# Cross-attention over 64 sequences: stores issued by ScalarE, fetches reordered on SyncE, the turn of the queries moved, the last scores in other PSUM banks

## The chip, the cores and the metric

The kernel runs on one core of a Trainium2 chip. The metric is the device time of one execution in microseconds. Five engines have instruction queues of their own: TensorE (PE, with its weight loads as PEld), VectorE (DVE), ScalarE (ACT), GpSimd (POOL) and SyncE (SP). SP and ACT also issue DMA transfers; SPq and ACTq in the profile are these issues.

## The reference

All is float32. x is 64 x 256 x 512, ctx is 64 x 256 x 384, the hidden width is 512.

```python
text_p  = einsum('bld,dh->blh', x, W_text)   + b_text
audio_p = einsum('bsd,dh->bsh', ctx, W_audio) + b_audio
Q = layer_norm(text_p, g1, beta1)
K = layer_norm(audio_p, g2, beta2)
V = audio_p
alpha = softmax(einsum('blh,bsh->bls', Q, K) / sqrt(512), axis=-1)
h = einsum('bls,bsh->blh', alpha, V)
h = einsum('blh,hk->blk', h, W_out) + b_out
return layer_norm(h + x, g_out, beta_out)
```

layer_norm takes mean and variance over the last axis, with 1e-5 added to the variance.

## The kernel before

**Work per sequence.** For each of the 64 sequences b (256 text rows and 256 audio rows, each as two tiles of 128 partitions) the kernel makes:

- the text projection q and the audio projection k. For b = 0 and 1 they are plain products (`multiply`, L314, product L317). For b from 2 on they are cut into blocks (class `Blocks`): seven products of block sums instead of eight products (`products`, L427), taken out of PSUM and added together by DVE (`leave`, one for each product, L438: the "sums" of the prediction). POOL makes the sums of the inputs (`sum_x`, `sum_c`, L271 to L289). A pool `p_pj` of four PSUM banks holds the products; two products share a bank.
- the LayerNorm of q and k without gain and shift: the squares (ACT, `square`, L335), 1/sqrt (POOL, `scales`, L297 and L299), the scaling of the rows (ACT, `normalise`, L363 or L365).
- the turn of the rows, so that the hidden axis lies on the partitions: the rows are stored to DRAM (`store`, L373, tiles qd and kd, 512 KB), fetched back as 32-wide squares (`fetch`, four DMAs of 128 KB by `squares`, L88, tiles qq and kq), and turned by DVE within 32 x 32 squares (`turn`: L91 for q, L394 for k). ACT applies gain and shift there (`affine`, L401, four instructions), giving qT and kT.
- the scores of 256 x 256 (L463) into a bank of `p_at` (two banks), their maxima (DVE, L473), the exponentials (ACT, L480). The exponentials take the same way through DRAM: stored as ed (`store_e`, L494, 256 KB), fetched in squares as eq (L88, 4 x 64 KB), turned by DVE (`turn_e`, L91).
- the context z = alpha times ctx (L525, two banks of `p_at` in turn, copied to zT by ACT, L532) and the output y (L542, into `p_y`, two banks), for which W_audio and W_out have been multiplied together beforehand (wao, `fold_multiply`, with the bias bao by `fold_bias`). DVE takes y out of PSUM and adds x (`evict`, L551), and does the last LayerNorm (`shift` L565, `settle` L570); the output rows are stored (L580).

x and ctx are loaded twice: as rows (`load_rows`, x 512 KB, c 384 KB) and as squares for the projections (`load_squares`, xq 4 x 128 KB, cq 4 x 96 KB; `turn_x`, `turn_c` on DVE).

**Order.** The order of every engine's queue is the order in which the code is written (`manual_schedule`, L65); nothing is rearranged. An engine works through its queue in order and waits where an operand or a buffer isn't ready. SP's queue holds all DMAs except the rows of biases and gains (`row`, L127) and five small vectors (`load_columns`), which ACT issues.

**The loop** (L693 to L771, b from 0 to 61) handles scores of b, context and output of b-1, the end of the LayerNorm of b-2, the projections of b+2, the squares of b+3 and b+4. In SP's order an iteration is: qq and kq of b+1 (L697, L698), ed of b, eq of b, xq and cq of b+4, x and c of b+1, the output of b-2, qd of b+2, kd of b+2. On DVE the turn of q[b+1] (L725) stands between sums 5 and 3 of the text projection; on PE all seven text products, the context of b-1 and the audio products follow each other, in the banks of `p_pj` and `p_at` that DVE and ACT empty.

**Before the loop** (L610 to L690) the weights are loaded and folded, the first two sequences are projected by plain products, and `turn_rows` (L167) turns c_0 and x_0 on PE. **After it** (L774 to L827) the last two sequences are finished; there the exponentials are turned on PE (`transpose_e`, L504).

Of the kernel before, what the change touches and what calls it, by code (L numbers as in the profile page):

```python
# [9 lines left out]
F32 = mybir.dt.float32  # L10
# [5 lines left out]
P = 128  # L16
SQ = 32
NQ = P // SQ
# [4 lines left out]
def kernel(  # L23
# [40 lines left out]
    nc = tc.nc  # L64
    ctx.enter_context(tc.manual_schedule())  # L65
    B, L, D = x.shape
    S, DA = c.shape[1:]
    H = w_text.shape[1]
    LT, ST = L // P, S // P
    DC, AC, HC = D // P, DA // P, H // P  # L70
    scale = 1.0 / math.sqrt(H)

    const = ctx.enter_context(tc.tile_pool(name="const", bufs=1))
# [6 lines left out]
    p_pj = ctx.enter_context(tc.tile_pool(name="p_pj", bufs=4, space=PSUM))  # L80
    p_at = ctx.enter_context(tc.tile_pool(name="p_at", bufs=2, space=PSUM))
# [14 lines left out]
    def load_squares(b):  # L96
        xq = blk.tile([P, L // SQ, D // NQ], F32, tag="xq", name=f"xq_{b}")
        cq = blk.tile([P, S // SQ, DA // NQ], F32, tag="cq", name=f"cq_{b}")
        squares(xq, x[b])
        squares(cq, c[b])  # L100
        return xq, cq
# [15 lines left out]
    def weight_by_square(w, chunks, name, queue):  # L117

        t = const.tile([P, chunks, H], F32, tag=name, name=name)
        v = w.rearrange("(q k i) h -> q i k h", q=NQ, i=SQ)  # L120
        for q in range(NQ):
            queue.dma_start(t[q * SQ : (q + 1) * SQ], v[q])
        return t

    def row(v, name):
        t = const.tile([P, H], F32, tag=name, name=name)
        nc.scalar.dma_start(t, v.rearrange("(o h) -> o h", o=1).broadcast_to([P, H]))  # L127
        return t

    vectors = const.tile([P, P], F32, tag="vectors", name="vectors")  # L130
    nc.vector.memset(vectors, 0.0)


    x_0 = xin.tile([P, LT, D], F32, tag="x", name="x_0")
    c_0 = cin.tile([P, ST, DA], F32, tag="c", name="c_0")
    nc.sync.dma_start(c_0, c[0].rearrange("(t p) d -> p t d", p=P))
    wa_sb = weight_by_square(w_audio, AC, "wa", nc.sync)
    ba_sb = row(b_audio, "ba")
    nc.sync.dma_start(x_0, x[0].rearrange("(t p) d -> p t d", p=P))
    wt_sb = weight_by_square(w_text, DC, "wt", nc.sync)  # L140
    blocks = {1: load_squares(1)}
    wo_sb = weight_by_square(w_out, HC, "wo", nc.sync)

    columns = const.tile([P, 5, HC], F32, tag="columns", name="columns")

    def load_columns():
        for n, v in enumerate((g1, beta1, g2, beta2, b_audio)):
            nc.scalar.dma_start(
                vectors[n * HC : (n + 1) * HC].rearrange("k (q i) -> k q i", q=NQ),
                v.rearrange("(q k i) -> k q i", q=NQ, i=SQ),  # L150
            )

    def take_columns():

        ps = p_at.tile([P, P], F32, tag="at", name="ps_v")
        nc.tensor.transpose(ps, vectors, ident)
        nc.scalar.copy(columns, ps[:, : 5 * HC].rearrange("p (n k) -> p n k", n=5))
        return [columns[:, n, :] for n in range(5)]
# [8 lines left out]
    def turn_rows(rows_sb, chunks, name, copy):  # L167

        ar = work.tile([P, 2, chunks, P], F32, tag="y" if chunks == DC else "kT", name=f"{name}r")
        T = work.tile([P, chunks, 2 * P], F32, tag=name, name=f"{name}_0")  # L170
        for t in range(2):
            arrange(ar[:, t], rows_sb[:, t, :], chunks, copy)
        for lo in range(0, chunks, 2):
            n = min(2, chunks - lo)
            ps = p_at.tile([P, 2, 2 * P], F32, tag="at", name="ps_rows")
            for j in range(n):
                for t in range(2):
                    nc.tensor.transpose(ps[:, j, bass.ts(t, P)], ar[:, t, lo + j, :], ident)
            nc.scalar.copy(T[:, lo : lo + n, :], ps[:, :n, :])
        return T  # L180

    def turn_weights():
# [119 lines left out]
    class Projection:  # L302
# [66 lines left out]
        def store(self):  # L369
            self.d = scratch.tile(  # L370
                [self.nt * P, H], F32, tag=f"{self.name}d", name=f"{self.name}d_{self.b}"
            )
            nc.sync.dma_start(self.d.rearrange("(t p) h -> p t h", p=P), self.rows)  # L373

        def fetch(self):
            self.sq = blk.tile(
# [77 lines left out]
    class Attention:  # L454
# [1 line left out]
            self.b, self.qT, self.kT = b, q.pop(b).T, k.pop(b).T  # L456
            self.xb, self.c_sb = rows[b]

        def scores(self):
            self.sc = p_at.tile([P, LT, S], F32, tag="at", name="ps_sc")  # L460
            for t in range(LT):
                for k in range(HC):
                    nc.tensor.matmul(  # L463
                        self.sc[:, t, :],
                        lhsT=self.qT[:, k, bass.ts(t, P)],
                        rhs=self.kT[:, k, :],
                        start=(k == 0),
                        stop=(k == HC - 1),
                    )
# [21 lines left out]

        def store_e(self):
            self.d = scratch.tile([L, S], F32, tag="ed", name=f"ed_{self.b}")
            nc.sync.dma_start(self.d.rearrange("(t p) s -> p t s", p=P), self.e)  # L494

        def fetch_e(self):
            self.sq = blk.tile([P, L // SQ, S // NQ], F32, tag="eq", name=f"eq_{self.b}")
# [4 lines left out]
            turn(self.eT, self.sq, ST)  # L502

        def transpose_e(self):  # L504
            self.ps_e = p_at.tile([P, ST, L], F32, tag="at", name="ps_e")
            for s in range(ST):
                for t in range(LT):
                    nc.tensor.transpose(
                        self.ps_e[:, s, bass.ts(t, P)], self.e[:, t, bass.ts(s, P)], ident
                    )  # L510
# [97 lines left out]


    cT[0] = turn_rows(c_0, AC, "cT", nc.vector.tensor_copy)  # L610
    bt_sb = row(b_text, "bt")
    load_columns()
    k[0] = audio(0, cT.pop(0))
    k[0].multiply(0)
    xT[0] = turn_rows(x_0, DC, "xT", nc.vector.tensor_copy)
# [16 lines left out]
    q[0].evict(1)  # L632
    q[0].scales()
    k[0].fetch()
    g1_sb, be1_sb, g2_sb, be2_sb, bac_sb = take_columns()

    for v in (g2_sb, be2_sb):
# [7 lines left out]
        k[1].multiply(t)  # L645
        k[1].evict(t)
    k[1].scales()
    bo_sb = row(b_out, "bo")
    k[1].normalise()
    q[0].fetch()  # L650
    k[1].store()
    blocks[2] = load_squares(2)
    k[1].fetch()
    k[0].turn()
    k[0].affine(g2_sb, be2_sb)
# [12 lines left out]
    q[1].normalise()  # L668
    q[1].store()
    q[1].fetch()  # L670
    q[0].affine(g1_sb, be1_sb)
    fold_evict(1)
    fold_multiply(2)
# [12 lines left out]
        wa_blocks[n].append(wa_sb[:, 2, k2 * H2 : (k2 + 1) * H2])  # L686
    cT[2] = turn_c(2)
    cs = {2: sum_c(cT[2])}
    go_sb = row(g_out, "go")
    beo_sb = row(beta_out, "beo")  # L690

    done = last = None
    for b in range(B - 2):  # L693
        three = b + 3 < B
        at = Attention(b)
        if b:
            q[b + 1].fetch()  # L697
            k[b + 1].fetch()  # L698
        at.scores()
        if done:  # L700
            done.evict(1)
            done.scales()
            done.shift(0)
        if last:
            last.turn_e()
        at.maxima()
        if done:
            done.shift(1)
        at.exponentials()
        at.store_e()  # L710
        at.fetch_e()
        if b + 4 < B:
            blocks[b + 4] = load_squares(b + 4)
        rows[b + 1] = load_rows(b + 1)
        q2 = q[b + 2] = Blocks("q", b + 2, xs.pop(b + 2), wt_blocks, bt_sb)
        q2.products(1, 2)
        q2.leave(1)
        if done:
            done.settle(0)
        q2.products(6, 5)  # L720
        q2.leave(6)
        q2.leave(2)
        q2.leave(5)
        q2.products(7, 3)
        q[b + 1].turn()  # L725
        q[b + 1].affine(g1_sb, be1_sb)
        q2.products(4)
        q2.leave(3)
        q2.leave(7)
        q2.leave(4)  # L730
        at.reciprocals()
        if last:
            last.context()
        q2.square()
        if done:
            done.settle(1)
            done.store()
        q2.scales()
        add_bias(b)
        k[b + 1].turn()  # L740
        k[b + 1].affine(g2_sb, be2_sb)
        q2.normalise()
        q2.store()
        k2 = k[b + 2] = Blocks("k", b + 2, cs.pop(b + 2), wa_blocks, ba_sb)
        k2.products(1, 2)
        k2.leave(1)
        k2.products(6, 5)
        k2.leave(6)
        k2.leave(2)
        k2.leave(5)  # L750
        k2.products(7, 3)
        k2.leave(3)
        k2.leave(7)
        k2.products(4)
        k2.leave(4)
        k2.square()
        k2.scales()
        if last:
            last.start_output()
            last.multiply(0)  # L760
        if three:
            xT[b + 3] = turn_x(b + 3)
            xs[b + 3] = sum_x(xT.pop(b + 3))
            cT[b + 3] = turn_c(b + 3)
            cs[b + 3] = sum_c(cT.pop(b + 3))
        k2.normalise()
        k2.store()
        if last:
            last.evict(0)
            last.multiply(1)  # L770
        done, last = last, at  # L771


    at = Attention(B - 2)  # L774
    q[B - 1].fetch()
    k[B - 1].fetch()
    rows[B - 1] = load_rows(B - 1)
    at.scores()
    done.evict(1)
# [21 lines left out]
    last.evict(1)  # L801
    last.scales()
    end = Attention(B - 1)
    end.scores()
    at.start_output()
    at.multiply(0)
    end.maxima()
# [52 lines left out]
```

## Time and profile before

| | |
|---|---|
| time, median of 3 runs | 1471.59 us (1470.97 to 1472.04) |
| profiled execution, in all | 1472.76 us |
| profiled execution, span of the profile | 1471.0 us |
| granted TensorE clock, mean | 0.995 |
| DMA moved | 322.41 MB, 219 GB/s on the mean |
| share of the 16 DMA engines' time, the queue of all these transfers | 76.7% |
| longest groups on PE | output y 340.3 us, scores 232.4 us, context 176.6 us |
| ACT, affine of qT and of kT | 132.9 and 132.2 us |

The profiled execution is one run; the median is of other runs, 1.2 us lower. A wait in the profile is the idle time of an engine ahead of an instruction, put down to what released it. A DMA's landing time runs from its issue to the moment when it is complete. Busy PE time is modelled from the starts of pipelined matmuls; the starts themselves are measured, so that distances between starts of the same operation in successive iterations are the safest measure of the loop's pace.

### The profile page before, as it was taken

Reading aid. Unit: us, or ns where it says so; the run is one execution under the profiler, and the core shown is the slowest. Engines: PE = TensorE matmul, PEld = TensorE weight load, DVE = VectorE, ACT = ScalarE, POOL = GpSimd, SP = SyncE. Lnnn points to the kernel's source line nnn. Section 1 sums busy time; section 2 is a strip of 40 time slices with the busy share of each in tenths; the row PEclk is TensorE's granted clock in tenths of the full one; section 3 lists DMA queues with packets and bytes.
Section 4 is the critical chain, followed back from the end, with each engine's and each line's share of the span. In section 5 each row is a group of like instructions: output and inputs, shape, how many; then the busy total and the mean of one; then the engine's idle time right before and its main releaser. Section 6 shows DMA issues by size and latency. Waiting matters only on the chain. (4 is left out here: it accounts for less than half of the span.)

```text
span 1471.0 us, 20463 instructions
## 1 busy us (share of the span) xinstructions
PE 1437.6 (98%) x5777; PEld 1097.4 (75%) x5777; DVE 1213.2 (82%) x2077; ACT 697.1 (47%) x1663; POOL 692.6 (47%) x1037
## 2 busy tenths in 40 slices
PE   7999999999999999999999999999999999999996
PEld 3577877877877777877877777777777777877873
DVE  4768888888888788888888797888888888888886
ACT  2435445445455355455455354355455355355352
POOL 1544454454454454454454453554554554454452
PEclk9999999999999999999999999999999999999999
DMA  8587777777787788887887777877877877878872
GB/s 193 151 223 204 225 233 213 230 234 205 242 241 201 236 236 207 240 233 208 237 243 199 238 231 201 242 209 226 245 223 211 246 232 214 239 216 224 241 217 80
DMA packets 450260, 322.41 MB, mean 219 GB/s; under 512 B 154724, under 2 KB 382564, under 8 KB 450148
## 3 DMA queue, kind: packets, MB, share of 16 engines
q1 hardware_dynamic: 449328, 319.79, 76.7%
q10 hardware_dynamic: 820, 1.32, 0.5%
q8 instruction: 47, 0.77, 0.2%
q14 instruction: 65, 0.53, 0.1%
HBM read 204.09 MB, written 116.92 MB: 218 GB/s over the span
## 5 line engine op out<-in xcount | busy, mean ns | idle before, releaser
L297 POOL TENSOR_SCALAR ve<-var 128x2 f32<-128x2 f32 x124 | 26.9, 217 | 680.3 <-ACT junk L335 680.3
L542 PE MATMUL ps_y<-wao,zT 128*128 128x512 f32 x768 | 340.3, 592 | 0.0
L401 ACT ACTIVATE qT<-qT,columns 128x256 f32<-128x256 f32 x256 | 132.9, 589 | 404.7 <-DVE qT L91 404.7
L542 PEld LDWEIGHTS ps_y<-wao,zT 128*128 128x128 f32 x768 | 145.8, 190 | 156.1 <-issue 142.8
L463 PEld LDWEIGHTS ps_sc<-kT,qT 128*128 128x128 f32 x1024 | 195.2, 191 | 55.1 <-issue 22.7
L463 PE MATMUL ps_sc<-kT,qT 128*128 128x256 f32 x1024 | 232.4, 380 | 1.5 <-ACT zT L532 1.5
L438 DVE TENSOR_TENSOR kr<-ps_k,kr 128x512 f32<-128x512 f32 x372 | 185.3, 512 | 24.7 <-DVE kr L438 0.9
L91 DVE STREAM_TRANSPOSE qT<-qq 128x1024 f32<-128x1024 f32 x64 | 79.7, 1245 | 151.0 <-DMA qq<-qd 151.0
L438 DVE TENSOR_TENSOR qr<-ps_q,qr 128x512 f32<-128x512 f32 x372 | 182.4, 504 | 14.7 <-PE ps_q L427 3.8
L525 PE MATMUL ps_z<-eT,c 128*128 128x256 f32 x768 | 176.6, 379 | 0.8 <-ACT eT L514 0.7
L480 ACT ACTIVATE e<-ps_sc,nmx 128x256 f32<-128x256 f32 x128 | 59.5, 469 | 238.0 <-DVE nmx L473 238.0
L427 PE MATMUL ps_q<-wtsum,xsum 128*128 128x256 f32 x744 | 170.7, 379 | 0.0
L427 PE MATMUL ps_k<-wa,cT 128*128 128x256 f32 x620 | 164.6, 380 | 0.0
L604 POOL TENSOR_TENSOR x<-x,bao 128x512 f32<-128x512 f32 x128 | 161.0, 1280 | 3.5 <-DMA x<-in_x_dram 3.5
L525 PEld LDWEIGHTS ps_z<-eT,c 128*128 128x128 f32 x768 | 145.8, 190 | 21.6 <-ACT eT L514 0.9
L427 PEld LDWEIGHTS ps_q<-wtsum,xsum 128*128 128x128 f32 x744 | 141.4, 190 | 19.2
L299 POOL TENSOR_TENSOR rstd<-ve,nhalf 128x2 f32<-128x2 f32 (+1 forms) x193 | 136.6, 708 | 16.0
L401 ACT ACTIVATE kT<-kT,columns 128x256 f32<-128x256 f32 x256 | 132.2, 591 | 3.4 <-DVE kT L91 3.4
L427 PEld LDWEIGHTS ps_k<-wa,cT 128*128 128x128 f32 x620 | 118.2, 191 | 16.2
L427 PE MATMUL ps_q<-wt,xT 128*128 128x256 f32 x496 | 117.2, 379 | 0.0
L363 ACT ACTIVATE kr<-kr,rstd 128x512 f32<-128x512 f32 x124 | 82.8, 715 | 69.9 <-POOL rstd L299 69.9
L427 PE MATMUL ps_k<-wasum,csum 128*128 128x256 f32 x372 | 102.6, 385 | 11.0 <-DVE qr L438 11.0
(113 smaller groups left out, 2228.6 us busy)
## 6 DMA issues: line engine op xcount, KB each, us to landing
x<-in_x_dram SPq DMA_DIRECT2D x64, 512.0 KB, 4.9
kd<-kr SPq DMA_DIRECT2D x64, 512.0 KB, 7.0
kq<-kd SPq DMA_DIRECT2D x256, 128.0 KB, 3.0
qd<-qr SPq DMA_DIRECT2D x64, 512.0 KB, 7.2
qq<-qd SPq DMA_DIRECT2D x256, 128.0 KB, 2.6
xq<-in_x_dram SPq DMA_DIRECT2D x252, 128.0 KB, 2.8
out_dram<-y SPq DMA_DIRECT2D x63, 512.0 KB, 6.0
c<-in_ctx_dram SPq DMA_DIRECT2D x64, 384.0 KB, 5.4
```

Of the source, the lines that this page charges most:

```text
L91: nc.vector.transpose(dst.rearrange("p k (b j) -> p b k j", j=SQ), src.rearrange("p b (k i) -> p b k i", k=chunks),)
L297: nc.gpsimd.tensor_scalar(ve, var, EPS, None, ALU.add)
L299: nc.gpsimd.tensor_tensor(r, ve, nhalf[:, :n], ALU.pow)
L363: nc.scalar.mul(row, row, self.r[t])
L401: nc.scalar.activation(self.T[:, k, :], self.T[:, k, :], AF.Identity, bias=bet[:, k : k + 1], scale=gam[:, k : k + 1],)
L427: nc.tensor.matmul(bank[:, j, :], lhsT=side, rhs=w, start=(i == 0), stop=(i == len(pairs) - 1))
L438: add = lambda o, i0, i1: nc.vector.tensor_tensor(o, i0, i1, ALU.add)
L463: nc.tensor.matmul(self.sc[:, t, :], lhsT=self.qT[:, k, bass.ts(t, P)], rhs=self.kT[:, k, :], start=(k == 0), stop=(k == HC - 1),)
L480: nc.scalar.activation(self.e[:, t, :], self.sc[:, t, :], AF.Exp, bias=self.nmx[:, t : t + 1], accum_out=self.den[:, t : t + 1],)
L525: nc.tensor.matmul(ps[:, j, :], lhsT=self.c_sb[:, s, bass.ts(lo + j, P)], rhs=self.eT[:, s, :], start=(s == 0), stop=(s == ST - 1),)
L542: nc.tensor.matmul(ps, lhsT=self.zT[:, k, bass.ts(t, P)], rhs=wao_sb[:, k, :], start=(k == 0), stop=(k == AC - 1),)
L604: nc.gpsimd.tensor_tensor(xb[:, t, :], xb[:, t, :], bao_sb, ALU.add)
```

## The change

1. The stores of q and k rows (qd, kd) and of the exponentials (ed) are issued by ACT instead of SP. The stores of the output stay on SP.
2. The fetches qq and kq follow their stores in the code, so that they stand at the end of an iteration in SP's queue, and not at the head of the next; ahead of the loop those of q[1] and k[1] already did.
3. Bias and gain rows are loaded by SP in place of ACT, at other points; the five small vectors are loaded by ACT at the start. c_0 is loaded in two halves, the second behind W_audio. The squares of sequence 2 are loaded earlier.
4. The turn and affine of q[b+1] move behind sums 3, 7 and 4 and behind the squares of q[b+2].
5. `turn_rows` fills one bank per half of the rows, instead of one per two chunks.
6. scores(63) and the PE transposes of the exponentials (`transpose_e`) use banks of `p_pj` instead of `p_at`.

```diff
     def row(v, name):
         t = const.tile([P, H], F32, tag=name, name=name)
-        nc.scalar.dma_start(t, v.rearrange("(o h) -> o h", o=1).broadcast_to([P, H]))
+        nc.sync.dma_start(t, v.rearrange("(o h) -> o h", o=1).broadcast_to([P, H]))
         return t
...
+    columns = const.tile([P, 5, HC], F32, tag="columns", name="columns")
+    for n, v in enumerate((g1, beta1, g2, beta2, b_audio)):
+        nc.scalar.dma_start(
+            vectors[n * HC : (n + 1) * HC].rearrange("k (q i) -> k q i", q=NQ),
+            v.rearrange("(q k i) -> k q i", q=NQ, i=SQ),
+        )
...
-    nc.sync.dma_start(c_0, c[0].rearrange("(t p) d -> p t d", p=P))
+    c_rows = c[0].rearrange("(t p) d -> p t d", p=P)
+    nc.sync.dma_start(c_0[:, :1], c_rows[:, :1])
     wa_sb = weight_by_square(w_audio, AC, "wa", nc.sync)
+    nc.sync.dma_start(c_0[:, 1:], c_rows[:, 1:])
     ba_sb = row(b_audio, "ba")
     nc.sync.dma_start(x_0, x[0].rearrange("(t p) d -> p t d", p=P))
     wt_sb = weight_by_square(w_text, DC, "wt", nc.sync)
+    bt_sb = row(b_text, "bt")
     blocks = {1: load_squares(1)}
     wo_sb = weight_by_square(w_out, HC, "wo", nc.sync)
+    bo_sb = row(b_out, "bo")
...
     def turn_rows(rows_sb, chunks, name, copy):
...
-        for lo in range(0, chunks, 2):
-            n = min(2, chunks - lo)
-            ps = p_at.tile([P, 2, 2 * P], F32, tag="at", name="ps_rows")
-            for j in range(n):
-                for t in range(2):
-                    nc.tensor.transpose(ps[:, j, bass.ts(t, P)], ar[:, t, lo + j, :], ident)
-            nc.scalar.copy(T[:, lo : lo + n, :], ps[:, :n, :])
+            ps = p_at.tile([P, chunks, P], F32, tag="at", name="ps_rows")
+            for j in range(chunks):
+                nc.tensor.transpose(ps[:, j, :], ar[:, t, j, :], ident)
+            nc.scalar.copy(T[:, :, bass.ts(t, P)], ps)
...
         def store(self):
-            nc.sync.dma_start(self.d.rearrange("(t p) h -> p t h", p=P), self.rows)
+            nc.scalar.dma_start(self.d.rearrange("(t p) h -> p t h", p=P), self.rows)
...
-        def scores(self):
-            self.sc = p_at.tile([P, LT, S], F32, tag="at", name="ps_sc")
+        def scores(self, end=False):
+            if end:
+                self.sc = p_pj.tile([P, LT, S], F32, tag="pj", name="ps_sc")
+            else:
+                self.sc = p_at.tile([P, LT, S], F32, tag="at", name="ps_sc")
...
         def store_e(self):
-            nc.sync.dma_start(self.d.rearrange("(t p) s -> p t s", p=P), self.e)
+            nc.scalar.dma_start(self.d.rearrange("(t p) s -> p t s", p=P), self.e)
...
         def transpose_e(self):
-            self.ps_e = p_at.tile([P, ST, L], F32, tag="at", name="ps_e")
+            self.ps_e = p_pj.tile([P, ST, L], F32, tag="pj", name="ps_e")
...
     k[0].fetch()
+    blocks[2] = load_squares(2)
     g1_sb, be1_sb, g2_sb, be2_sb, bac_sb = take_columns()
...
     k[1].store()
-    blocks[2] = load_squares(2)
     k[1].fetch()
...
     q[1].fetch()
+    go_sb = row(g_out, "go")
+    beo_sb = row(beta_out, "beo")
     q[0].affine(g1_sb, be1_sb)
...
     for b in range(B - 2):
...
-        if b:
-            q[b + 1].fetch()
-            k[b + 1].fetch()
         at.scores()
...
         q2.products(7, 3)
+        q2.leave(3)
+        q2.leave(7)
+        q2.products(4)
+        q2.leave(4)
+        q2.square()
         q[b + 1].turn()
         q[b + 1].affine(g1_sb, be1_sb)
-        q2.products(4)
-        q2.leave(3)
-        q2.leave(7)
-        q2.leave(4)
         at.reciprocals()
         if last:
             last.context()
-        q2.square()
...
         q2.normalise()
         q2.store()
+        q2.fetch()
...
         k2.normalise()
         k2.store()
+        k2.fetch()
...
     at = Attention(B - 2)
-    q[B - 1].fetch()
-    k[B - 1].fetch()
...
     end = Attention(B - 1)
-    end.scores()
+    end.scores(end=True)
```

More of the change, by code (lines that the diff above doesn't have):

```diff
@@ L140 @@
     wt_sb = weight_by_square(w_text, DC, "wt", nc.sync)
+    bt_sb = row(b_text, "bt")
     blocks = {1: load_squares(1)}
     wo_sb = weight_by_square(w_out, HC, "wo", nc.sync)
[L144 to L151, printed above, removed]
+    bo_sb = row(b_out, "bo")
     def take_columns():
@@ L610 @@
     cT[0] = turn_rows(c_0, AC, "cT", nc.vector.tensor_copy)
-    bt_sb = row(b_text, "bt")
-    load_columns()
     k[0] = audio(0, cT.pop(0))
@@ L647 @@
     k[1].scales()
-    bo_sb = row(b_out, "bo")
     k[1].normalise()
@@ L688 @@
     cs = {2: sum_c(cT[2])}
-    go_sb = row(g_out, "go")
-    beo_sb = row(beta_out, "beo")
     done = last = None
```

## The prediction

> **What bounds the kernel now.** I read the busy totals first, then the waits of PE (TensorE), DVE (VectorE) and SP (SyncE), then the timeline round one stall, then the clock by stage.
>
> ```profile
> PE 1437.6 (98%) x5777; PEld 1097.4 (75%) x5777; DVE 1213.2 (82%) x2077; ACT 697.1 (47%) x1663; POOL 692.6 (47%) x1037
> ```
> PE is busy for 98% of the span, so at most some 33 us can be had. Where does PE wait?
> ```profile
> PE ps_k L427 <- DVE qr L438: 11.0, 11, 3.1
> PE ps_sc L463 <- ACT zT L532: 1.5, 1, 1.5
> ```
> (waited for: us in all, times, longest.) 11.0 us go to the audio products, which need a PSUM bank that a text sum on DVE has not yet emptied. The timeline shows why (start, duration, engine, operation, wait before it):
> ```profile
> 977.89 1.25 DVE L91 STREAM_TRANSPOSE qT<-qq 128x1024 f32<-128x1024 f32 x1 [3.51 <-DMA qq<-qd]
> ...
> 979.06 1.64 DVE L438 TENSOR_TENSOR qr<-ps_q,qr 128x256 f32<-128x256 f32 x3
> ...
> 980.32 0.67 PE L427 MATMUL ps_k<-wasum,csum 128*128 128x256 f32 x2 [0.39 <-DVE qr L438]
> ...
> 982.55 5.31 PE L542 MATMUL ps_y<-wao,zT 128*128 128x512 f32 x12
> ...
> 993.12 0.65 DVE L473 TENSOR_REDUCE nmx<-ps_sc 128x2 f32<-128x512 f32 x1
> ```
> DVE stands 3.51 us before the turn of q, which waits for the fetched squares qq; the last three sums stand behind it, and PE behind them. Over the run DVE waits thus for 151 us, but PE has slack: the starts of the scores lie 21.98 or 21.99 us apart in 48 of 60 iterations (1009.69, 1031.67, 1053.66). Only 12, all before 990, are longer, by 7.7 us in all: from scores(2) at 100.64 to scores(62) at 1427.40 the mean is 22.11. Two early stalls cost more:
> ```profile
> 68.45 1.19 PE L427 MATMUL ps_k<-wasum,csum 128*128 128x256 f32 x2 [2.88 <-DVE qr L438]
> ...
> 91.60 1.19 PE L427 MATMUL ps_k<-wasum,csum 128*128 128x256 f32 x2 [3.11 <-DVE qr L438]
> ```
> Two matmuls took 1.19 us after these pauses and 0.67 after the pause of 0.39 above: the clock had dropped.
> ```profile
> 66.00:88.00 22.00, 19.55 (x77) 16.76 (x78) 12.94 (x22) 10.07 (x24) 9.11 (x14) 0.84 0.77 206
> 88.00:110.00 22.00, 18.89 (x69) 13.83 (x68) 18.64 (x31) 10.82 (x26) 10.87 (x16) 0.92 0.81 217
> ```
> (PE, PEld, DVE, ACT, POOL busy; clock; DMA share; GB/s.) The granted clock was 0.84 and 0.92, against 1.00 later. Last, SP:
> ```profile
> SPq L88 <- DMA qd<-qr: 312.3, 63, 6.7
> SPq L88 <- DMA ed<-e: 165.4, 62, 3.1
> ...
> SPq L88 <- DMA go<-in_L_xattn_g_out_dram: 9.7, 1, 9.7
> ```
> SP stands still while stores land, and every load queued behind waits too. The third row is the odd one: square loads waited 9.7 us for a bias row that they don't use. The order and waits of the built program explain it: all transfers take eight completion semaphores in turn, and a transfer waits until its semaphore's last user has landed.
>
> **Turn behind the sums.** Nothing is added: sums 3, 7, 4 (1.64 us) and the two squares (0.63 each, ACT) go ahead of the turn. The bank waits go: 7.7 us in the loop, of which I count 7.6, and in the first two iterations 2.88 + 3.11, by starts 3.0 + 3.3, plus 3.0 + 2.0 of half clock (matmuls at twice the interval, 0.43 instead of 0.22 us): 11.3. What is late next is y, which needs zT, whose copies stand behind the affine of q on ACT. With x the start of the turn, T that of y: 1.28 to the affine (977.89 to 979.17), 2.08 for it and 0.82 for the copies, so x must be at T-4.2 or earlier. Before, it was at T-4.66.
>
> **Stores on ACT, fetches after them.** Three issues per iteration (0.4 us each) move from SP to ACT, 1.2 us on an engine busy for 47%; this is free as long as ACT's idle time covers it, and would otherwise be 1.2 us x 60 = 72. SP issues out, then qq and kq, at the end of the iteration instead of the head of the next. The eight semaphores are now shared by two engines, which adds waits. On ACT, kd waits for the first quarter of eq (behind it: exponentials, ed), ed for qd (behind it: squares, affine, zT), qd for the first quarter of kq (behind it: the squares of k). These had landed by then in before's order of times: 0. On SP, c waits for kd (behind it: out, qq), and **the third quarter of qq waits for ed**. That closes a ring through the iteration:
>
> - the turn 1.17 us (977.89 to 979.06), then DVE's work from the reciprocal at 980.62 to the maxima at 993.12, 12.50: 13.67;
> - maxima and exponentials 1.70 (993.12 to 994.82);
> - ed lands: median 3.2, from 2.9 (shortest) to 6.0 (out's median, when much is in flight);
> - third and fourth quarter of qq: 0.45 to issue, then 2.6 (median), from 2.1 to 3.0 (kq's median); the turn follows.
>
> ```profile
> ed<-e SPq DMA_DIRECT2D x62, 256.0 KB, 3.2
> eq<-ed SPq DMA_DIRECT2D x248, 64.0 KB, 2.0
> ```
> Sum at medians: 13.67 + 1.70 + 3.2 + 0.45 + 2.6 = 21.62 us, just under PE's 21.98. Between 20.8 and 24.8 everything is possible; I take the medians, as these are the same transfers. Then the loop runs at 21.98.
>
> The page "DMA: Bandwidth & Descriptors" of the Trainium skill, section "Issuing engines are not separate DMA queues", says that all issuers share the same 16 DMA engines, and that issuing from several saves only sequencer time. The rows above put SP's loss in standing still, not in issuing, so a second issuer may be worth more than the rule allows; by the rule alone the stores would bring 0, and the sum stays as it is, since I give them nothing.
>
> **Prologue.** Here the shared semaphores cost. The third quarter of cq_1 now waits for kd_0. Before, kd_0 was issued at 25.03; a store of that size took 4.06 us from issue to the fetch that waits for it (33.45 to 37.51). 25.0 + 4.1 + 0.45 + 2.9 (cq's landing) + 0.94 (turn) = 33.4, where PE began k[1] at 30.15: 3.3 of idle. The pause is as long as the two above, so half clock: 2.0 to 3.0, I take 2.3. The last half of cq_2 and then qq_0 wait for kd_1: qq_0 lands at 54 to 57 (before some 42), and the second fold copy stands behind q[0]'s affine on ACT: about 2.8 of idle before the bias fold. Scores(1) wait about 2.0. In b = 1 qq_2 waits for ed_1, which waits for kd_2: turn at about 95 and y(0) some 6 us late, with the clock included. Sum 3.3 + 2.3 + 2.8 + 2.0 + 6.0 = 16.4 added, 11.3 removed: **+5.1**. Bounds: none of the waits bites fully, -3; twice the clock losses, +8. Bias rows and vectors on other queues, c_0 in halves (first products at 10.3 to 12.2 instead of 11.62) and the six transposes in another grouping: 0, from -1 to +1, because wa and wt, not they, ended PE's waits there (1.3 and 0.9 us); all of it is inside these bounds.
>
> **Last scores.** scores(63) waited 1.50 us for a p_at bank:
> ```profile
> 1443.66 3.72 PE L463 MATMUL ps_sc<-kT,qT 128*128 128x256 f32 x16 [1.50 <-ACT zT L532]
> ```
> In p_pj, idle by then, they follow ps_z at once, and everything to the end follows them: -1.6 by starts (1442.0 instead of 1443.66). Bounds -2.4 (the 0.68 us wait for eT goes too) and 0.
>
> **Sum.** Against the profiled execution (span 1471.0, 1472.76 in all): -7.6 + 5.1 - 1.6 = -4.1, 1468.7. The median shown is 1.2 below that execution: **1467.5**.
>
> **Rivals.**
> 1. *The ring of ed and qq sets the pace* (slower). Place: the third quarter of qq behind ed. Decisive point: ed and qq together over 21.98 - 15.82 = 6.16 us, against 5.8 at medians. For it: ed now starts while c (384 KB), out (512 KB) and two quarters of qq are in flight, and out's median is 6.0; DMA engines are at 77%. Against: ed's longest wait before was 3.1. With ed at 4.5 the period is 22.92, that is 0.81 over mean before, x 60 = +48.6: 1471.6 + 48.6 + 5.1 - 1.6 = 1524; with 3.7, 22.12: +0.6, 1475.7. I hold 22.05 to 23.4, 1471 to 1552.
> 2. *The change doesn't do what it says*: loads still arrive late now and then, the stalls come back as waits for zT, and the mean stays 22.11: 1471.6 + 5.1 - 1.6 = 1475.
> 3. *The prologue gains instead*: stores land in 3 us, the new waits hardly bite, -3: 1471.6 - 7.6 - 3 - 1.6 = 1459.4.
>
> **How the numbers follow.** A difference below 0.2% (2.9 us) can hardly be told from none: faster is below 1468.6, slower above 1474.5. Forecast (PE's pace, prologue -1 to +8, 1461 to 1471): 0.50, of which 0.36 faster, 0.14 same. Rival 1: 0.30, 0.27 slower, 0.03 same. Rival 2: 0.10, half same, half slower. Rival 3: 0.10, faster. Together 0.46, 0.22, 0.32. The range starts at 1456, a little under rival 3, and reaches to 1515, which leaves out the upper third of rival 1 (0.10). The likeliest case's own range is 1461 to 1471.
>
> **What would show it.** Right: no row of PE's waits for ps_k on qr; scores 21.98 apart throughout; scores(2) at 104 to 108 instead of 100.64; a gap before k[1] near 31 us; scores(63) directly behind ps_z. Wrong: a wait of ps_y for zT in every iteration with SP's fetch of qq waiting for ed (rival 1: ed's landing above 3.6 us), or k[1] at 30 and scores(2) at 98 (rival 3). The forecast hangs most on 0.36 us of slack in the ring, multiplied by 60.

## The result and the profile after

The changed kernel takes 1595.03 us (median of 4 runs, 1590.02 to 1598.19), the kernel before 1471.82 in the same comparison: ratio 1.0826, 95% interval 1.0789 to 1.0864. The prediction was 1467.5 with a range of 1456 to 1515: wrong in sign and outside the range.

Where do the 122.3 us between the two spans (1593.3 and 1471.0) lie? The starts of the scores cut the execution in three:

| | before | after | difference | predicted |
|---|---|---|---|---|
| start to scores(2) | 100.64 | 103.85 | +3.2 | +5.1 |
| scores(2) to scores(62), 60 iterations | 22.11 each | 24.13 each | +120.9 | -7.6 |
| scores(62) to the end | 43.60 | 41.77 | -1.8 | -1.6 |

Everything is in the loop. First the page and PE's waits in the changed kernel:

```profile
PE 1471.0 (92%) x5777; PEld 1099.9 (69%) x5777; DVE 1234.3 (77%) x2077; ACT 718.2 (45%) x1663; POOL 698.8 (44%) x1037
```
```profile
PE ps_y L544 <- ACT zT L534: 97.9, 52, 5.7
```

The wait of ps_k for a text sum, 11.0 us before, is gone, as predicted. In its place PE waits for zT in nearly every iteration (52 times, 97.9 us). Behind that stands the turn of q, which on VectorE now waits 199.8 us for qq (151.0 before). And why is qq late? SyncE's waits (waited for: us in all, times, longest):

```profile
SPq L107 <- DMA kd<-kr: 475.9, 59, 9.1
SPq L88 <- DMA ed<-e: 219.5, 62, 6.0
SPq L88 <- DMA qd<-qr: 34.9, 5, 8.3
```

The wait that qq really needs, for qd, is almost nothing. What SyncE waits for is kd, 8.1 us per iteration, ahead of the load of c (L107), which has no use for kd; and ed, 3.5 us, ahead of a quarter of qq, which has no use for ed. One iteration in SyncE's and ScalarE's queues, from the timeline:

```profile
988.06 1.25 DVE L91 STREAM_TRANSPOSE qT<-qq 128x1024 f32<-128x1024 f32 x1 [3.01 <-DMA qq<-qd]
...
991.94 5.42 PE L544 MATMUL ps_y<-wao,zT 128*128 128x512 f32 x12 [1.68 <-ACT zT L534]
...
993.80 0.39 SPq L106 DMA_DIRECT2D x<-in_x_dram  x1
...
999.63 0.37 ACTq L372 DMA_DIRECT2D kd<-kr  x1
...
1002.20 0.65 DVE L475 TENSOR_REDUCE nmx<-ps_sc 128x2 f32<-128x512 f32 x1
...
1002.68 0.39 SPq L107 DMA_DIRECT2D c<-in_ctx_dram  x1
...
1003.15 0.46 SPq L582 DMA_DIRECT2D out_dram<-y  x1
...
1003.70 6.02 SPq L88 DMA_DIRECT2D qq<-qd  x4
...
1003.94 0.37 ACTq L496 DMA_DIRECT2D ed<-e  x1
```

c is issued 8.9 us behind x, as soon as kd has landed; out and qq stand behind it. The four issues of qq take 6.02 us instead of 1.8, because the third waits for ed. The next turn starts at 1011.90. So the ring that the prediction drew closes: 14.14 from turn to maxima, 1.74 to the issue of ed, 5.78 to the end of the issues of qq, 2.18 to the turn: 23.84 us, against PE's 21.98. The sum at the medians of before had been 21.62.

The trace also names the semaphore that tells of each landing. In the changed kernel eight semaphores carry all transfers of SyncE and ScalarE. In each of the 50 iterations between 200 and 1400 us, c takes the semaphore that kd used last, and the third quarter of qq the one that ed used last. In the 25 of them where the landing is known, c is issued 0.06 us after kd has landed and the third quarter 0.02 us after ed has, on the median.

### The profile page after: what moved, and what is told of

It is laid out like the page before. It is cut to its first block, busy times and chain, and to the rows that moved or that the text cites. A ratio compares the mean times of both kernels' runs of the same rounds, so it can differ in the third digit from the quotient of the medians.

```text
span 1593.3 us, 20278 instructions
## 1 busy us (share of the span) xinstructions
PE 1471.0 (92%) x5777; PEld 1099.9 (69%) x5777; DVE 1234.3 (77%) x2077; ACT 718.2 (45%) x1663; POOL 698.8 (44%) x1037
## 4 chain that ended last, share of the span: by engine, by line
DVE 36%; DMA 29%; PE 13%; ACT 6%; SPq 6%; issue 4%; DVEq 0%; POOL 0%; POOLq 0%; ACTq 0%
DMA ed<-e 18%; DVE kr L437 9%; PE ps_y L544 8%; DMA kq<-kd 7%; SPq L88 6%; DVE st L236 4%; DMA qq<-qd 4%; DVE y L553 4%; DVE xT L91 3%; PE ps_sc L465 3%; ACT qT L400 3%; DVE kT L393 3%; DVE y L567 3%; DVE cT L91 3%; ACT e L482 3%
## 5 line engine op out<-in xcount | busy, mean ns | idle before, releaser
L544 PE MATMUL ps_y<-wao,zT 128*128 128x512 f32 x768 | 369.4, 633 | 98.1 <-ACT zT L534 97.9
L544 PEld LDWEIGHTS ps_y<-wao,zT 128*128 128x128 f32 x768 | 149.4, 201 | 288.6 <-issue 148.8
L91 DVE STREAM_TRANSPOSE qT<-qq 128x1024 f32<-128x1024 f32 x64 | 79.7, 1245 | 199.8 <-DMA qq<-qd 199.8
L334 ACT ACTIVATE junk<-qr 128x512 f32<-128x512 f32 x124 | 78.1, 630 | 265.0 <-DVE qr L437 265.0
L572 DVE SCALAR_TENSOR_TENSOR y<-y,rstd,beo 128x512 f32<-128x512 f32 x128 | 99.6, 778 | 34.6 <-POOL rstd L298 33.5
```

The costliest lines, as they stand in the source:

```text
L91: nc.vector.transpose(dst.rearrange("p k (b j) -> p b k j", j=SQ), src.rearrange("p b (k i) -> p b k i", k=chunks),)
L544: nc.tensor.matmul(ps, lhsT=self.zT[:, k, bass.ts(t, P)], rhs=wao_sb[:, k, :], start=(k == 0), stop=(k == AC - 1),)
L572: nc.vector.scalar_tensor_tensor(self.y[:, t, :], self.y[:, t, :], self.r[t], beo_sb, ALU.mult, ALU.add)
```

## Experiments

Every ratio is to the kernel before, timed together with it; its time was 1472 to 1490 there, by chip. Where a kernel was run once, there is no interval. The profile of before is from the chip where it took 1472 us. The period is the mean distance of scores(2) to scores(62) in the profiled execution. "The tie" is a transfer that waits for an unrelated one because both use the same completion semaphore, or because it stands behind such a one in SyncE's queue. The semaphores are taken in turn, so an edit that moves a transfer or its issuer can also change which transfers share one; in e3 the ties are those of the changed kernel.

**e1: ed back on SyncE.** One line of the changed kernel:

```diff
-            nc.scalar.dma_start(self.d.rearrange("(t p) s -> p t s", p=P), self.e)
+            nc.sync.dma_start(self.d.rearrange("(t p) s -> p t s", p=P), self.e)
```

> The changed kernel with one line back: the exponentials (ed) are stored by SyncE, the q and k rows still by ScalarE. Theory A (the ring: the third quarter of qq shares a completion semaphore with ed and waits for its landing): in this program's order ed stands behind qq and kq, no quarter of qq waits for ed, the ring is open; the loop falls from 24.13 to PE's 21.98, time 1463 to 1475. Theory B (stores issued by a second engine collide with the loads on the 16 DMA engines, whoever waits for whom): two of the three stores are still on ScalarE, so most of the loss stays; period above 23, time above 1530. Theory C (the turn behind the sums makes zT late): nothing changes, about 1595.

Measured 1608.2, ratio 1.079 (1.070 to 1.088), period 24.23. Theory A in this form fell: opening the ring through ed gave nothing. The next one was there already:

```profile
1004.30 5.30 SPq L88 DMA_DIRECT2D cq<-in_ctx_dram  x4
1009.71 0.39 SPq L106 DMA_DIRECT2D x<-in_x_dram  x1
1014.14 0.39 SPq L107 DMA_DIRECT2D c<-in_ctx_dram  x1
1014.62 0.42 SPq L582 DMA_DIRECT2D out_dram<-y  x1
1015.09 2.91 SPq L88 DMA_DIRECT2D qq<-qd  x4
```

cq is held until qd has landed, c until kd has (issued at 1009.55); then x, c, out and qq go within some 8 us of each other and share the DMA engines. qq's landing rose to 4.8 us (2.6 before). The time also fits theory B (above 1530), and nearly theory C (about 1595), which falls with e7.

**e2: ed on GpSimd** (the same line with `nc.gpsimd`).

> The changed kernel with ed stored by GpSimd. Its transfers have completion semaphores of their own, so no load waits for ed, but ed starts at the same moment as in the changed kernel, beside c, out and qq. Theory A: the ring is open though ed's landing stays long (above 4 us); period 21.98 to 22.3, time 1465 to 1495, unless the issue on GpSimd takes long. Theory B: ed collides as before, period about 24, time 1580 to 1600.

1613.1, period 24.35. Here out waits for kd (333.8 us), and cq for qd. The time is above what either theory wanted, and nearer to theory B, which was to be taken seriously from here on. GpSimd's transfers do have semaphores of their own in the trace: eight that no transfer of SyncE or ScalarE uses.

**e3: half of the output store.** It leaves the second 128 rows of each output unwritten.

```diff
-                out[self.b].rearrange("(t p) d -> p t d", p=P)[:, lo : lo + n],
-                self.y[:, lo : lo + n],
+                out[self.b].rearrange("(t p) d -> p t d", p=P)[:, lo : lo + 1],
+                self.y[:, lo : lo + 1],
```

> The changed kernel, but each store of the output writes the first 128 of 256 rows only (256 KB in place of 512); order, waits and number of transfers stay. It tells why ed lands after 4.8 us. If ed shares the DMA engines with out and c, which are issued 0.8 and 1.3 us ahead of it: ed's landing falls by 0.5 to 1.0 us (a store of 512 KB took 4.06 us and one of 256 KB 3.0 when alone, so 256 KB are worth 1.0), period 23.1 to 23.6, time 1533 to 1565. If ScalarE's own queue is slow whatever runs beside it: ed stays at 4.8, time 1590 to 1600.

1560.4, period 23.50, as expected of shared DMA engines:

```profile
ed<-e ACTq DMA_DIRECT2D x62, 256.0 KB, 4.8
...
ed<-e ACTq DMA_DIRECT2D x62, 256.0 KB, 3.9
```

(the changed kernel, then e3; in us from issue to landing, on the median). 256 KB less beside ed took 0.9 us off its landing and 0.6 off the period. Of the 1.6 us that ed's landing had gained over before, this shows a little more than half to be a sharing of the DMA engines with out. ScalarE's queue as such is not slow: in e13 and e14 ed, issued there too, landed after 3.2 and 2.3.

**e4: maxima first.** `at.maxima()` ahead of `done.shift(0)` and `last.turn_e()`.

> The changed kernel with the maxima on VectorE ahead of shift(0) and the turn of e, so that the exponentials start earlier; in this program's order the second quarter of qq, not the third, waits for ed. Theory A: the maxima come 12.7 instead of 14.1 us behind the turn of q, and one more quarter is issued behind ed, so the ring is 12.7 + 1.7 + 4.85 + 0.9 + 2.76 = 22.9; time 1595 - 60 x 1.2 = 1522 (1505 to 1540). Theories B and C have no ring through the maxima: 1595, within 10.

1660.4, period 25.13: worse, where theory A wanted 1522. The maxima did come earlier, but c still waited for kd (295.6 us), whose landing was now 5.7 us (2.8 in the changed kernel): cq is held by qd here, and x goes out beside kd. Opening the ring at one place did not help; the place that binds moved.

**e5: only the q rows on ScalarE**, the rest on SyncE.

> The changed kernel with ed and the k rows stored by SyncE again; only the q rows are stored by ScalarE. Opening the ring of ed alone gave nothing: the trace of that kernel shows the next one, c waiting for kd through the shared semaphore, with out and qq behind it (kd is issued 11.6 us behind the turn of q and lands 4.6 later, then 0.95 + 2.5 + 4.15 to the next turn: 23.8). Theory A2 (any wait of SyncE's load queue for a late ScalarE store closes a ring): in this program cq waits for qd, which is issued 7.3 us behind the turn and lands at 10.7; then cq, x, c, out, qq: the next turn could come at 17.5, so no ring binds. Period 21.98 to 22.1, time 1463 to 1480. Theory B (stores from a second engine collide with loads, whoever waits): a third of the stores is still there, so about a third of the loss: 1500 to 1520. Theory C (the turn behind the sums makes zT late): above 1580.

1586.1, ratio 1.066 (1.060 to 1.072). Missed by the second form of theory A too: I had looked for a ring through qq only. Here kd stands behind qq in SyncE's queue, lands after 6.0 us beside x, c and out, and the turn of k waits for kq (186.4 us, against 22.9 in the changed kernel).

**e6 and e9: all three stores on GpSimd.** In the changed kernel, both lines:

```diff
-            nc.scalar.dma_start(self.d.rearrange("(t p) h -> p t h", p=P), self.rows)
+            nc.gpsimd.dma_start(self.d.rearrange("(t p) h -> p t h", p=P), self.rows)
...
-            nc.scalar.dma_start(self.d.rearrange("(t p) s -> p t s", p=P), self.e)
+            nc.gpsimd.dma_start(self.d.rearrange("(t p) s -> p t s", p=P), self.e)
```

> The changed kernel with all three stores issued by GpSimd, whose transfers have completion semaphores of their own: no load waits for a store that it doesn't need, while the stores start when they did. Theory A2: no ring but the true ones (qd to qq, 7.3 + 3.5 + 1.4 + 3 = 15 us; kd to kq, 11.6 + 4 + 1.9 + 3 = 20.5, against 21.98 + 2.4): period 21.98 to 22.3, time 1465 to 1495, if GpSimd's own work (693 us before) leaves room for the issues. Theory B: about 24, time 1580 to 1620.

> The kernel with all three stores on GpSimd again, now timed against the kernel before. One look gave 1451.4 with PE's pace of 21.98 in the whole loop. Theory A2: ratio to before 0.970 to 0.988, no spread from the loop.

1451.43 in one run, then 1451.54 (5 runs, 1450.28 to 1452.06), ratio 0.982 (0.980 to 0.984): the fastest kernel of this study, 1.8% faster than before (with everything else of the change in it too). 59 of 60 distances of the scores are 21.98 or 21.99. As in e2, GpSimd's transfers have eight semaphores of their own, so no load shares one with a store of q, k or e. The timeline of e9 shows what that frees:

```profile
1003.76 1.91 SPq L88 DMA_DIRECT2D xq<-in_x_dram  x4
1005.77 1.87 SPq L88 DMA_DIRECT2D cq<-in_ctx_dram  x4
1007.75 0.39 SPq L106 DMA_DIRECT2D x<-in_x_dram  x1
1008.24 0.41 SPq L107 DMA_DIRECT2D c<-in_ctx_dram  x1
1008.75 0.42 SPq L582 DMA_DIRECT2D out_dram<-y  x1
```

xq, cq, x, c and out follow each other without a gap, and are issued at least 7 us ahead of the next qq (1015.94), which waits for qd alone.

**e7: the turn alone.** The kernel before with only this edit:

```diff
-        q[b + 1].turn()
-        q[b + 1].affine(g1_sb, be1_sb)
-        q2.products(4)
         q2.leave(3)
         q2.leave(7)
+        q2.products(4)
         q2.leave(4)
+        q2.square()
+        q[b + 1].turn()
+        q[b + 1].affine(g1_sb, be1_sb)
         at.reciprocals()
         if last:
             last.context()
-        q2.square()
```

> The kernel before with the turn and affine of q moved behind the sums and squares, nothing else. By the prediction's step: -7.6 in the loop and -11.3 in the first two iterations, 1450 to 1460 where before is 1472 (ratio 0.985 to 0.993), no wait of ps_k for qr. By theory C the late zT takes its place: waits of ps_y for zT of 1 us or more per iteration, ratio above 1.02. Where q's squares come late now and then, some of the gain may return as waits of ps_y for zT: ratio 0.993 to 1.0.

Ratio 0.998 (0.996 to 1.001): nothing that can be measured, where the prediction's step wanted 0.985 to 0.993; 0.993 to 1.0 had been named for the case that the gain returns as waits for zT. Theory C, which wanted more than 1.02, is refuted. The bank waits are gone, and this stands in their place:

```profile
PE ps_y L542 <- ACT zT L532: 21.8, 20, 4.0
```

32 of 60 iterations ran at PE's pace, the others waited for zT. The step was right in its mechanism, and its gain went to the next wait, because SyncE's queue still brought qq late (VectorE waits 108.5 us for it). How many such waits the kernel before has on this chip, where it took 1487 us, was not traced.

**e8: all of the change but the stores and the fetches** (both as before).

> The changed kernel with all stores on SyncE and the fetches at the head of the iteration, as before: the new order of loads ahead of the loop, the turn behind the sums and the last scores in p_pj stay. Theories A2 and B both take the loss away here: period 21.98 to 22.1, ratio to before 0.980 to 0.995 (-7.6 loop, -11.3 first iterations, -1.6 end, 0 to +5 ahead of the loop). Theory C: ratio above 1.05.

Ratio 0.992 (0.989 to 0.996). scores(2) starts at 91.03, in e7 at 98.75: without stores on ScalarE, what the change does ahead of the loop (the new order of loads and `turn_rows`) is worth 7.7 us by these two profiled executions, on one chip. The loop is that of e7, 22.40.

**e10: one tie put back.** In e9's kernel, a read of 128 bytes of kd ahead of c, with c, out and qq behind it:

```diff
         k2.store()
+        nc.sync.dma_start(peek, k2.d[0:1, 0:32])
+        nc.sync.dma_start(c_sb, c[b + 1].rearrange("(t p) d -> p t d", p=P))
+        if done:
+            done.store()
+        q2.fetch()
         k2.fetch()
```

(the loads and stores named are taken away at their earlier places).

> The kernel with all stores on GpSimd, and one tie put back by hand: SyncE reads 128 bytes of kd ahead of c, so that c, out, qq and kq stand behind kd's landing, as the shared semaphore made them in the changed kernel; nothing else is different but that 128-byte read. Theory A2: the ring kd, c, out, qq, turn is closed again (11.6 + 4 to 6 + 1.0 + 1.4 to 2.5 + 3.4 to 4.2 = 21.4 to 25.3, with the kernels that had this ring at 23.8 to 24.4), time 1540 to 1615. Theory B (stores of ScalarE collide, GpSimd's don't): 1450 to 1460.

1734.3, period 26.47: no store on ScalarE, and slower by 283 us than e9 on the same chip, and by 139 us than the changed kernel on another. The read waits 825.8 us in all. So the holding of SyncE's queue is enough to make such a loss, and theory B (1450 to 1460) fails here. The size was more than expected (1540 to 1615); GpSimd issues kd later, 14.9 us behind the turn on the median, ScalarE 11.6 in the changed kernel.

**e11 and e12: one store on ScalarE, two on GpSimd**: the q rows, or the k rows.

> The q rows are stored by ScalarE, the k rows and ed by GpSimd. In this program the last quarter of cq waits for qd, which is issued 7.3 us behind the turn. Theory A2: landing at about 11, then cq, x, c, out, qq: the turn could come at 18, so no ring binds: 1450 to 1465. Theory B: one store of three on ScalarE, a third of the loss, 1485 to 1510, the same as its twin with the k rows.

> The k rows are stored by ScalarE, the q rows and ed by GpSimd. In this program c waits for kd, which is issued 11.6 us behind the turn, with out, qq and kq behind it. Theory A2: ring of 23 to 25 us, time 1540 to 1615. Theory B: one store of three on ScalarE, 1485 to 1510, the same as its twin with the q rows.

1508.5 (period 22.88) and 1495.3 (22.39). Both lie about where theory B put them, and outside what A2 foretold. The timeline of e11 tells why A2 was wrong about it:

```profile
1004.75 6.18 SPq L88 DMA_DIRECT2D cq<-in_ctx_dram  x4
1011.04 0.39 SPq L106 DMA_DIRECT2D x<-in_x_dram  x1
1011.53 0.41 SPq L107 DMA_DIRECT2D c<-in_ctx_dram  x1
1012.04 0.42 SPq L584 DMA_DIRECT2D out_dram<-y  x1
1012.51 3.06 SPq L88 DMA_DIRECT2D qq<-qd  x4
```

cq is held until qd has landed. That closes no ring, but x, c and out now go directly ahead of qq, where in e9 they had gone 7 us earlier: qq lands after 6.3 us (2.6 in e9) and kd after 5.7 (4.1), and the turn of k waits 143.5 us. In e12 the ring through kd exists, and is short, since kd lands after 2.8 us where I had counted 4 to 6. Yet c waits for kd in it as long as in the changed kernel:

```profile
SPq L107 <- DMA kd<-kr: 484.8, 59, 9.3
```

So the length of that wait does not tell what it costs.

**e13 and e14: all stores on ScalarE, other loads behind them.** Theories A and B still stood apart; this pair keeps the stores of the changed kernel and all transfers, and moves only `load_squares(b + 4)`: behind `q2.fetch()` in e13, behind `k2.fetch()` in e14.

```diff
-        if b + 4 < B:
-            blocks[b + 4] = load_squares(b + 4)
         rows[b + 1] = load_rows(b + 1)
...
         q2.fetch()
+        if b + 4 < B:
+            blocks[b + 4] = load_squares(b + 4)
```

> The changed kernel, all three stores on ScalarE, with the squares xq and cq loaded behind the fetch of qq and not behind eq; same transfers, same bytes. In this program no transfer ahead of qq waits for a store that it doesn't need: kd's semaphore goes to the last quarter of xq, ed's to the third of cq, both behind qq; kq stands behind them. Theory A3 (a load that waits for a ScalarE store holds back all that SyncE has behind it): x, c, out and qq go in time; what is left is kq behind ed: 15.8 + 3.2 to 4.5 + 0.9 + 2.3 + 2.8 = 25.0 to 26.3, against 21.98 + 2.4 that the turn of k allows: period 22.6 at most to 23.9, at best 21.98, time 1460 to 1560. Theory B (the stores of ScalarE collide with loads wherever these wait): as the changed kernel, 1585 to 1605.

> Its twin: xq and cq loaded behind the fetch of kq. In this program kd's semaphore goes to c, ahead of out and qq, ed's to the last quarter of kq, qd's to eq. Theory A3: the hold of c by kd is back, 11.3 + 2.8 to 4.6 + 1.0 + 1.4 to 2.5 + 3.4 to 4.3 = 19.9 to 23.7, and the turn of k waits for ed as well (15.8 + 3.2 to 4.5 + 0.5 + 2.8 = 22.3 to 23.6, against 24.4); slower than its twin by 10 to 60 us, 1500 to 1590. Theory B: no difference between the twins, both 1585 to 1605.

1505.4 and 1629.8 on one chip, where before took 1489.8 (all single runs): 124 us between two kernels with the same stores on the same engine. In e13 nothing ahead of qq waits for a store, but that of qd; qq lands after 2.6 us, as before, and ed after 3.2, as before:

```profile
1002.12 0.39 SPq L106 DMA_DIRECT2D x<-in_x_dram  x1
1002.60 0.41 SPq L107 DMA_DIRECT2D c<-in_ctx_dram  x1
1003.11 0.42 SPq L582 DMA_DIRECT2D out_dram<-y  x1
1011.56 2.37 SPq L88 DMA_DIRECT2D qq<-qd  x4
1013.98 1.96 SPq L88 DMA_DIRECT2D xq<-in_x_dram  x4
1015.98 5.00 SPq L88 DMA_DIRECT2D cq<-in_ctx_dram  x4
```

Here the hold by ed falls on cq (5.00 instead of 1.9), and kq behind it costs the rest (161.3 us of waiting before the turn of k). In e14 the hold by qd falls on eq and that by kd on c:

```profile
1012.44 6.82 SPq L88 DMA_DIRECT2D eq<-ed  x4
1019.37 0.39 SPq L106 DMA_DIRECT2D x<-in_x_dram  x1
1025.46 0.39 SPq L107 DMA_DIRECT2D c<-in_ctx_dram  x1
1025.94 0.42 SPq L582 DMA_DIRECT2D out_dram<-y  x1
1026.41 2.86 SPq L88 DMA_DIRECT2D qq<-qd  x4
```

Theory B, which wanted both at 1595, is refuted. e13 lay where theory A3 wanted it (1460 to 1560), e14 above (1500 to 1590).

## Why the prediction was wrong

**The step that failed is "Stores on ACT, fetches after them", and in it the term "ed lands: median 3.2".** The step named the right waits and the right ring, and priced them too low.

*The ring through ed and qq* was drawn, and its sum was 21.62 us, with landing times taken from before "as these are the same transfers". On the medians of the changed kernel it measures 23.78:

| | prediction | changed kernel |
|---|---|---|
| turn to maxima | 13.67 | 14.14 |
| maxima to the issue of ed | 1.70 | 1.73 |
| ed lands | 3.2 | 4.76 |
| third and fourth quarter of qq issued | 0.45 | 0.37 |
| fourth quarter's issue to the turn | 2.6 | 2.78 |

ed is 1.6 us of the 2.2. The 0.47 ahead of the maxima is the turn of k, which waits for kq (0.48 us in the iteration shown). The landing of qq was sized rightly where it counts. The median over all four quarters did rise, from 2.6 to 3.5:

```profile
qq<-qd SPq DMA_DIRECT2D x256, 128.0 KB, 3.5
```

But the third and the fourth quarter, which close the ring, landed after 2.4 and 2.7; the first two, which go out right behind c and out, after 4.6 and 5.1. The bytes of ed were the same, the neighbours weren't: e3 shows it (half of out away: 4.8 to 3.9).

*c waits for kd (behind it: out, qq)* was named and priced at nothing. It is SyncE's largest wait, 475.9 us, but this is not its price, as e12 shows. What it does in the changed kernel is to send c and out 1.3 and 0.8 us ahead of ed, so that ed lands late. And where ed is set free (e1), this hold, with that of cq by qd ahead of it, closes a ring of its own.

Rival 1 was the right case. I had closed it at 23.4 and given it 0.30, because the slack of 0.36 us at the medians looked like a forecast, when it hung on durations that the change itself alters. With the measured landings, 4.8 and 2.7, its formula gives 15.82 + 7.5 = 23.3 us, inside its range; the mean period, 24.13, lies above it, by the turn of k and by single iterations of up to 27.6. Rival 1 was also incomplete: it is not one ring, but a queue in which any hold can be paid, as e1, e5 and e11 showed against my own later forms of the theory.

**The turn behind the sums**: the mechanism was right (no wait of ps_k in the changed kernel), the size not. -7.6 and -11.3 were counted; alone it gave 0.998 (e7), as the wait for zT that the prediction named as "late next" took its place. That zT had 0.5 us of room on the profiled iteration was worked out there, and not used.

**Prologue** +3.2 against +5.1: near, and in part by terms that offset each other. PE waited 2.59 us before k[1] (3.3 foretold), 2.42 before the bias fold (2.8) and 5.70 before y(0), with half clock behind it (6.0 foretold for both); the 2.0 of scores(1) did not come. **Last scores** -1.8 against -1.6: right. In the changed kernel scores(63) follow the context directly:

```profile
1563.54 2.75 PE L527 MATMUL ps_z<-eT,c 128*128 128x256 f32 x12
1566.13 3.62 PE L465 MATMUL ps_sc<-kT,qT 128*128 128x256 f32 x16
```

**One issuer or several.** The page "DMA: Bandwidth & Descriptors" of the Trainium skill, section "Issuing engines are not separate DMA queues", says that several issuers save only the time on the sequencer. I held against it that SyncE's loss lay in standing still. With ScalarE the second issuer gained nothing here, and the change lost 8.3%. With GpSimd e9 is 1.8% faster than before. 0.8% of this came with e8 already, which moves no store (on another chip); the other 1% or so, for the same transfers, goes with stores that no longer hold loads and with the new place of the fetches, which were not separated.

**What stays open.** How much of the 2.15 us per iteration is the hold itself and how much the bunch behind it is not separated: no run holds the queue without bunching it. Half of out explains 0.9 of the 1.6 us of ed's landing; whether c explains the rest was not tried. That the eight semaphores are the tie rests on the semaphores, the order and SyncE's waits in the traces, and on e10 and e13/e14; the number of semaphores itself was not varied.

## What to carry to other kernels

Before moving a store to another issuing engine, list for every load what it will wait for, the completion semaphore's last user included, and everything that stands behind it in the same queue; a load that waits for a late store holds all of them. Don't price a transfer by its median from before when the change alters what is in flight beside it: put the slack of the ring beside the spread of the landing times, and if the spread is larger, forecast the ring. The longest wait of a queue need not be the costly one: follow the ring that binds. For the same stores, an issuer with semaphores of its own (here GpSimd) gave a kernel 1.8% faster than before; one that shares them (ScalarE) gave one 8% slower, or about 1% where only the place of two other loads was changed (e13, one run).

## What the runs showed of the hardware

- The landing of one and the same transfer differs from kernel to kernel, with what is in flight beside it, far more than expected: the output store of 512 KB took 2.7 us on the median in e10, 4.3 in the changed kernel and 6.5 in e9; a quarter of qq (128 KB) 2.6 to 6.3. Within the changed kernel the second quarter of qq took 5.1 and the third 2.4.
- A store issued by GpSimd took 0.77 us of it, one issued by ScalarE 0.37 of its queue. GpSimd's busy time was 698.8 us in the changed kernel and 883.9 in e9, of which 147 are the stores, and PE kept its pace.
- Shorter pauses of PE than the two early ones can cost clock too. For the 61 groups of 12 matmuls of y that start between 96 and 1551 us in the changed kernel, the time from the first start to the next group's start was:

| pause before y, us | groups | 5.15 to 5.25 us | 6.8 to 6.95 us |
|---|---|---|---|
| up to 1.93 | 41 | 41 | 0 |
| 1.96 to 2.58 | 15 | 6 | 9 |
| from 2.80 on | 5 | 0 | 5 |

In the slow ones some of the matmuls start 0.85 us apart instead of 0.43; one of them (pause 2.45) has a granted clock of 0.78 from 1500 to 1507 us, against 1.00 from 1490 to 1497. The page "TensorE: Matmul & The Clock Gate" of the Trainium skill, Part 1, gives an idle window of about 3.4 us for the clock to drop, and says that the window runs free of the kernel. The free window fits the mixed middle row; but pauses of 1.96 to 3.05 us are shorter than the window that the page names, and cost clock here.
